# Deformable sampling as TensorE products with hat weights instead of row gathers, on one Trainium2 core

## The chip, the cores and the metric

The kernel runs on one core of one Trainium2 chip. The metric is the device time of one execution in microseconds (us). In the profile PE is TensorE's matmul, PEld its weight load, DVE is VectorE, ACT is ScalarE, POOL is GpSimd, SP is SyncE; a "q" behind a name (SPq) is that engine's DMA queue. The clock in a table is the share of its full clock that TensorE was granted. "L369" is line 369 of that kernel's own source, so the same statement has other numbers in the variants below.

## The reference

Two layers over `x` of shape [2, 256, 128, 128], all fp32. The first normalises `x` by groups, computes for three branches (dilation 1, 9, 12) offsets by a 3x3 convolution, samples the image bilinearly at nine shifted taps, weights the taps per channel, and applies a LayerNorm over the channels and a gelu. The sum of the branches and of a 1x1 convolution passes through a LayerNorm, an MLP and a last LayerNorm. The second layer is a ternary 3x3 convolution.

```python
def _deform_dw(x, offset, w, pad, dil):
    off = offset.reshape(B, 9, 2, H, W)
    py = yy - pad + ky * dil + off[:, :, 0]
    px = xx - pad + kx * dil + off[:, :, 1]
    sampled = _bilinear(x, py, px)                 # 4 corners per tap, zero outside the image
    return jnp.einsum('bckhw,ck->bchw', sampled, w.reshape(C, 9))

def _branch(x, w_off, w_def, lw, lb, pad, dil):
    off = _conv(x, w_off, pad, dil)
    y = _deform_dw(x, off, w_def, pad, dil)
    return gelu(_ln2d(y, lw, lb))                  # LayerNorm over the 256 channels of a pixel
# ... (cut)
out = _ln2d(x1 + x2 + x3 + conv1x1(x), n1_w, n1_b)
out = _ln2d(mlp(out) + out, n2_w, n2_b)
```

## The kernel before

Pixels lie on the 128 partitions, channels along the free axis. For each of 27 taps of each image row, one indirect DMA on GpSimd gathers the four corners of 128 pixels (4 KB each) from a table. ACT and DVE blend them with per-pixel weights, DVE multiplies by the tap's weights, and TensorE adds the nine taps in PSUM.

```python
# per tap (phase_b), 2 x 128 x 27 = 6912 times
nc.scalar.activation(s, G[:, 0:C], AF.Copy, scale=wt[:, 0:1])
for j in range(1, 4):
    nc.vector.scalar_tensor_tensor(s, G[:, j * C : (j + 1) * C], wt[:, j : j + 1], s, ALU.mult, ALU.add)
nc.vector.tensor_tensor(sw, s, defw[:, tap, :], ALU.mult)
ins = nc.tensor.matmul(y, lhsT=ident, rhs=sw, start=kt == 0, stop=kt == 8)
advance()      # one step of LayerNorm, gelu and MLP of an earlier row
```

With pixels on the partitions a LayerNorm needs one number for each partition, so the inverse square root runs on GpSimd over one column:

```python
def rsqrt(dst, var, eps):
    nc.gpsimd.tensor_scalar(ve, var, eps, None, ALU.add)
    nc.gpsimd.tensor_tensor(dst, ve, mhalf[:, :n], ALU.pow)      # n = 1 (2 for group norms)
```

The offsets of image 1 and the last convolution of image 0 are traced beside the sampling (`together`); the rest of the kernel is not needed here.

Of the kernel before, what the change touches and what calls it, by code (L numbers as in the profile page):

```python
# [10 lines left out]
I32 = mybir.dt.int32  # L11
# [10 lines left out]
KC = C // P          # channel chunks  # L22
HID = 512
MC = HID // P
R = 4                # image rows per group
NG = R * W           # pixels per group
PAD = 12             # widest reach of the offset convolutions
WP = W + 2 * PAD
DILS = (1, 9, 12)
NTAP = 27            # 3 branches x 9 taps  # L30
NOFF = 2 * NTAP
NPLAN = 5 * NTAP     # 4 corner weights and one index per tap
TW = W + 2           # the sampling table has a row per (floor(y) + 1, floor(x) + 1)
AHEAD = 7            # gathers issued ahead of the tap that uses them
GBUFS = 9
LOAD_AT = 64         # the tap of a group at which the next group's loads are issued
# [3 lines left out]
# 0.05 in float32, its two 12-bit halves, and half a unit in its last place  # L40
# [7 lines left out]
def conv_preact_kernel(ctx: ExitStack, tc: tile.TileContext, t: dict, out: bass.AP):  # L48
    nc = tc.nc
    x = t["x"]  # L50
    NB, _, H, _ = x.shape
    NGRP = H // R
    HALO = PAD // R      # groups of rows on either side that an offset convolution reaches
    TH = H + 2
# [3 lines left out]
    small = ctx.enter_context(tc.tile_pool(name="small", bufs=6))  # L58
    ps_tp = ctx.enter_context(tc.tile_pool(name="ps_tp", bufs=2, space=PSUM))
    ps_mm = ctx.enter_context(tc.tile_pool(name="ps_mm", bufs=2, space=PSUM))  # L60

# [1 line left out]
    ident = const.tile([P, P], F32, name="ident")  # L63
    make_identity(nc, ident)
    mhalf = const.tile([P, 2], F32, name="mhalf")
    nc.vector.memset(mhalf, -0.5)
    ones = const.tile([1, P], F32, name="ones")
    nc.vector.memset(ones, 1.0)

    def load(name, shape, src):  # L70
# [5 lines left out]
    offw = load("offw", [P, KC, 9, NOFF], t["offw"].rearrange("(k p) t n -> p k t n", p=P))  # L76
# [3 lines left out]
    convb = load("convb", [1, C], t["convb"])  # L80
    b2 = load("b2", [1, C], t["b2"])
    b1 = load("b1", [P, MC], t["b1"])
    n1w = load("n1w", [P, KC], t["n1w"])
# [4 lines left out]
    defw = load("defw", [P, NTAP, C], t["defw"].partition_broadcast(P))  # L88
    bw = load("bw", [P, 3, C], t["bw"].partition_broadcast(P))
    bb = load("bb", [P, 3, C], t["bb"].partition_broadcast(P))  # L90

# [1 line left out]
    table = [  # L93
        scratch.tile([TH * TW, 4 * C], F32, name=f"table{b}", tag=f"table{b}") for b in range(NB)
    ]
    plan = [scratch.tile([H, W, NPLAN], F32, name=f"plan{b}", tag=f"plan{b}") for b in range(NB)]
    x1d = [scratch.tile([C, H * W], F32, name=f"x1d{b}", tag=f"x1d{b}") for b in range(NB)]

    # Work for TensorE that runs beside a main stream is issued behind this instruction of it.
    fence = None  # L100

    def behind(ins):
        if fence is not None:
            tc.add_manual_dep(
                ins.ins,
                fence.name,
                mybir.DependencyInfo(
                    mybir.DependencyClass.NoSync, mybir.DependencyReason.DATA
                ),
                reason="beside the main stream",  # L110
            )

# [1 line left out]
    def rsqrt(dst, var, eps):  # L114
        """dst = (var + eps) ** -0.5"""
        n = var.shape[1]
        ve = small.tile([P, n], F32, name="ve", tag="ve")
        nc.gpsimd.tensor_scalar(ve, var, eps, None, ALU.add)  # L118
        nc.gpsimd.tensor_tensor(dst, ve, mhalf[:, :n], ALU.pow)  # L119

    def group_norm(stats, name):
        """Per channel mean and rstd of its group of 8 channels; stats [P, KC, n, 6]."""
        mv = small.tile([P, KC, 2], F32, name="gnmv", tag="gnmv", bufs=2)
        for k in range(KC):
            nc.vector.bn_aggr(mv[:, k, :], stats[:, k].rearrange("p n s -> p (n s)"))  # L125
        mean = const.tile([P, KC], F32, name=f"{name}_mean", tag=f"{name}_mean")
        rstd = const.tile([P, KC], F32, name=f"{name}_rstd", tag=f"{name}_rstd")
        pm = ps_mm.tile([P, 512], F32, name="gnps", tag="mm")
        nc.tensor.matmul(pm[:, 0:KC], lhsT=gmask, rhs=mv[:, :, 0], start=True, stop=True)
        nc.vector.tensor_copy(mean, pm[:, 0:KC])  # L130
        d = small.tile([P, KC], F32, name="gnd", tag="gnd", bufs=2)
        nc.vector.tensor_tensor(d, mv[:, :, 0], mean, ALU.subtract)
        nc.vector.tensor_tensor(d, d, d, ALU.mult)
        nc.vector.tensor_tensor(d, d, mv[:, :, 1], ALU.add)
        pv = ps_mm.tile([P, 512], F32, name="gnps", tag="mm")
        nc.tensor.matmul(pv[:, 0:KC], lhsT=gmask, rhs=d, start=True, stop=True)
        var = small.tile([P, KC], F32, name="gnvar", tag="gnvar", bufs=2)
        nc.vector.tensor_copy(var, pv[:, 0:KC])
        rsqrt(rstd, var, GN_EPS)
        return mean, rstd  # L140

    def ln_stats(src):
        """Mean and rstd of each row of src [P, C]."""
        st = small.tile([P, 6], F32, name="lnst", tag="lnst")
        nc.vector.bn_stats(st, src)  # L145
        mv = small.tile([P, 2], F32, name="lnmv", tag="lnmv")
        nc.vector.bn_aggr(mv, st)  # L147
        rs = small.tile([P, 1], F32, name="lnrs", tag="lnrs")
        rsqrt(rs, mv[:, 1:2], LN_EPS)
        return mv, rs  # L150
# [3 lines left out]

    gn1 = []
    with tc.tile_pool(name="gnload", bufs=2) as gp:
        XT = min(8, NGRP)
        for b in range(NB):
            stats = gp.tile([P, KC, NGRP, 6], F32, name="stats1", tag="stats1")
            for k in range(KC):  # L160
                for g0 in range(0, NGRP, XT):
                    n = min(XT, NGRP - g0)
                    xt = gp.tile([P, XT * NG], F32, name="xt", tag="xt")
                    nc.sync.dma_start(
                        xt[:, : n * NG],
                        x[b, k * P : (k + 1) * P].rearrange("p h w -> p (h w)")[
                            :, g0 * NG : (g0 + n) * NG
                        ],
                    )
                    for j in range(n):  # L170
                        nc.vector.bn_stats(stats[:, k, g0 + j, :], xt[:, j * NG : (j + 1) * NG])
            gn1.append(group_norm(stats, f"gn1_{b}"))

# [1 line left out]
    def phase_a(b, pool, ps_off, ring, base):  # L175
        mean, rstd = gn1[b]
        tv = table[b].rearrange("(y x) (s c) -> y x s c", x=TW, s=4)

        # The border of the table, where a corner lies outside the image.
        zero = base["zero"]  # L180
        for dy in range(2):
            for yy in (0, H + 1) if dy == 0 else (H, H + 1):
                row = tv[yy, :, 2 * dy : 2 * dy + 2, :].rearrange("(q j) s c -> q j (s c)", j=2)
                for j in range(2):
                    nc.sync.dma_start(row[:, j], zero[0 : TW // 2])
            for dx in range(2):
                for xx in (0, W + 1) if dx == 0 else (W, W + 1):
                    nc.sync.dma_start(
                        tv[1 - dy : 1 - dy + H, xx, 2 * dy + dx, :], zero[0:H, 0:C]
                    )  # L190
        yield

        def load_group(g):
            for k in range(KC):
                nc.sync.dma_start(
                    ring[g % len(ring)][:, k, :, PAD : PAD + W],
                    x[b, k * P : (k + 1) * P, g * R : (g + 1) * R, :],
                )

        def normalise_group(g):  # L200
            for k in range(KC):
                xk = ring[g % len(ring)][:, k, :, PAD : PAD + W]
                normalise(xk, xk, mean[:, k : k + 1], rstd[:, k : k + 1])

        def tabulate(g):
            xp = ring[g % len(ring)]
            ts = pool.tile([P, R, C], F32, name="ts", tag="ts", bufs=2)
            for h in range(R // 2):
                tp = ps_tp.tile([P, 512], F32, name="tpa", tag="tp")
                for j in range(2):  # L210
                    for k in range(KC):
                        behind(
                            nc.tensor.transpose(  # L213
                                tp[:, (j * KC + k) * P : (j * KC + k + 1) * P],
                                xp[:, k, 2 * h + j, PAD : PAD + W],
                                ident,
                            )
                        )
# [547 lines left out]
```

## Time and profile before

| | us |
|---|---|
| median time (19012.79 to 19031.13) | 19021.79 |
| offsets of image 0, TensorE alone | to about 2400 |
| sampling of both images, DVE 81 to 87% busy | about 15,500 |
| last convolution of image 1 | about 1,070 |

### The profile page before, as it was taken

How to read it: one execution, taken by the hardware profiler on the slowest of the kernel's cores; microseconds unless marked ns; L12 is line 12 of the kernel's file. 1: busy time of each engine (PE TensorE's matmuls, PEld its weight loads, DVE VectorE, ACT ScalarE, POOL GpSimd, SP SyncE). 2: the span in 40 equal slices, each digit the busy share in tenths (PEclk: the TensorE clock that was granted, in tenths of full speed). 3: DMA queues.
4: the chain of work that ended last, by engine and by line, in shares of the span. 5: the costliest groups of instructions: out<-in, count | busy, mean ns of one | idle time of the engine just before them, and what ended most of it. 6: DMA issues, size and time to landing. Idle time of an engine off the chain costs nothing. (4 is left out here: it accounts for less than half of the span.)

```text
span 19048.3 us, 184576 instructions
## 1 busy us (share of the span) xinstructions
PE 15534.4 (82%) x52208; PEld 10999.5 (58%) x52208; DVE 13137.0 (69%) x35538; ACT 4065.9 (21%) x8322; POOL 9696.9 (51%) x9511
## 2 busy tenths in 40 slices
PE   7999998898989988888666677777777777777799
PEld 7999997777777777776333333333333344333344
DVE  2000017878777878888888888888888888888600
ACT  0000002222222222222222222222222222222100
POOL 0000005656555565666666666666666666666400
PEclk9855555666666666666666677777877777787899
DMA  4110127777777777777777777777778787888511
GB/s 145 32 40 31 37 71 241 244 243 251 241 245 245 241 247 247 245 242 248 262 259 260 244 257 262 260 263 258 261 259 263 257 264 260 267 263 261 179 39 37
DMA packets 1347582, 4036.18 MB, mean 212 GB/s; under 512 B 126946, under 2 KB 392292, under 8 KB 1344116
## 3 DMA queue, kind: packets, MB, share of 16 engines
q0 software_dynamic: 995328, 3624.32, 58.2%
q1 hardware_dynamic: 216052, 265.81, 4.1%
q10 hardware_dynamic: 135168, 134.23, 2.1%
q8 instruction: 408, 6.68, 0.1%
q14 instruction: 626, 5.13, 0.1%
HBM read 3800.61 MB, written 223.25 MB: 211 GB/s over the span
## 5 line engine op out<-in xcount | busy, mean ns | idle before, releaser
L359 POOL DMA_INDIRECT G<-table,plb x6912 | 8428.6, 1219 | 7312.3 <-DVE sw L502 2651.4
L498 DVE SCALAR_TENSOR_TENSOR s<-G,plb,s 128x256 f32<-128x256 f32 x20736 | 8855.1, 474 | 92.3 <-ACT s L496 90.4
L505 PE MATMUL y<-sw,ident 128*128 128x256 f32 x13824 | 6050.8, 552 | 2851.1 <-DVE sw L502 2841.0
L505 PEld LDWEIGHTS y<-sw,ident 128*128 128x128 f32 x13824 | 3141.6, 260 | 5205.4 <-DVE sw L502 4533.5
L496 ACT ACTIVATE s<-G,plb 128x256 f32<-128x256 f32 x6912 | 3414.4, 506 | 10383.7 <-DVE sw L502 10285.2
L248 PEld LDWEIGHTS po<-offw,ring 128*128 128x128 f32 x24544 | 5112.8, 311 | 192.5 <-issue 16.3
L248 PE MATMUL po<-offw,ring 128*128 128x18 f32 (+1 forms) x24544 | 4895.1, 356 | 4.0 <-DVE pos L281 4.0
L502 DVE TENSOR_TENSOR sw<-s,defw 128x256 f32<-128x256 f32 x6912 | 2807.5, 415 | 1.9
L609 PE MATMUL pc<-cring,wq 128*128 128x512 f32 x4608 | 2526.9, 694 | 55.5 <-DVE o L621 53.1
L270 DVE TENSOR_TENSOR pos<-po,pos 128x27 f32<-128x27 f32 x256 | 32.6, 177 | 2528.2 <-PE po L248 2528.2
L609 PEld LDWEIGHTS pc<-cring,wq 128*128 128x128 f32 x4608 | 1040.2, 227 | 1111.6 <-issue 929.1
L145 DVE BATCH_NORM_STATS2 lnst<-y 128x6 f32<-128x256 f32 x768 | 329.3, 429 | 939.0 <-PE y L505 930.5
L118 POOL TENSOR_SCALAR ve<-lnmv 128x1 f32<-128x1 f32 x1280 | 462.0, 361 | 762.7 <-DVE lnmv L147 689.5
L153 DVE TENSOR_SCALAR a<-y,lnmv,lnrs 128x256 f32<-128x256 f32 x768 | 416.3, 542 | 626.2 <-POOL lnrs L119 621.7
L119 POOL TENSOR_TENSOR lnrs<-ve,mhalf 128x1 f32<-128x1 f32 x1280 | 798.3, 624 | 67.3
L403 PE MATMUL S<-ge,ident 128*128 128x256 f32 x1536 | 734.3, 574 | 82.0 <-ACT ge L402 69.6
L621 DVE SCALAR_TENSOR_TENSOR o<-pc,l1b,xl 128x512 f32<-128x512 f32 x128 | 95.5, 746 | 840.7 <-PE pc L609 840.7
L219 ACT COPY ts<-tpa 128x512 f32<-128x512 f32 x128 | 74.1, 586 | 2500.5 <-PE tpa L213 2487.8
L438 PE MATMUL hp<-oT,w 128*128 128x512 f32 x1024 | 569.0, 681 | 0.7 <-ACT oT L424 0.7
L403 PEld LDWEIGHTS S<-ge,ident 128*128 128x128 f32 x1536 | 373.9, 279 | 335.5 <-ACT ge L402 246.8
L461 PE MATMUL h<-w,hT 128*128 128x256 f32 x2048 | 524.5, 389 | 0.0
L379 PE MATMUL S<-convb,ones 1*128 1x256 f32 x512 | 280.5, 644 | 207.5 <-DVE n L153 198.7
(98 smaller groups left out, 5523.1 us busy)
## 6 DMA issues: line engine op xcount, KB each, us to landing
table<-ts ACTq DMA_DIRECT2D x256, 512.0 KB, 6.8
G<-table,plb POOLq DMA_INDIRECT x6912, 5.5
xl<-x1d SPq DMA_DIRECT2D x120, 384.0 KB, 6.9
xt<-in_x SPq DMA_DIRECT2D x16, 2048.0 KB, 7.3
ring<-in_x SPq DMA_DIRECT2D x128, 256.0 KB, 3.9
xg<-in_x SPq DMA_DIRECT2D x64, 512.0 KB, 8.3
x1d<-x SPq DMA_DIRECT2D x64, 512.0 KB, 5.0
out_x<-o SPq DMA_DIRECT2D x128, 256.0 KB, 2.1
```

The source lines that it names most:

```text
L118: nc.gpsimd.tensor_scalar(ve, var, eps, None, ALU.add)
L119: nc.gpsimd.tensor_tensor(dst, ve, mhalf[:, :n], ALU.pow)
L248: nc.tensor.matmul(po[:, r * NOFF + n0 : r * NOFF + n0 + n], lhsT=xp[:, k, yy % R, PAD + dx : PAD + dx + W], rhs=offw[:, k, tap, n0 : n0 + n],
L359: nc.gpsimd.indirect_dma_start(out=G, out_offset=None, in_=table[b], in_offset=bass.IndirectOffsetOnAxis(ap=groups[g]["plan"][:, r, 4 * NT ...
L403: nc.tensor.matmul(gr["S"][r], lhsT=ident, rhs=ge, start=False, stop=br == 2)
L438: nc.tensor.matmul(hp, lhsT=w1[:, k, m * P : (m + 1) * P], rhs=oT[:, k, :], start=k == 0, stop=k == KC - 1,)
L461: nc.tensor.matmul(h2, lhsT=hT[:, m, cols], rhs=w2[:, m, :], start=False, stop=m == MC - 1)
L496: nc.scalar.activation(s, G[:, 0:C], AF.Copy, scale=wt[:, 0:1])
L498: nc.vector.scalar_tensor_tensor(s, G[:, j * C : (j + 1) * C], wt[:, j : j + 1], s, ALU.mult, ALU.add)
L502: nc.vector.tensor_tensor(sw, s, defw[:, tap, :], ALU.mult)
L505: ins = nc.tensor.matmul(y, lhsT=ident, rhs=sw, start=kt == 0, stop=kt == 8)
L609: nc.tensor.matmul(pc, lhsT=wq[:, k, ky * 3 + kx, m * P : (m + 1) * P], rhs=xc[:, k, ky : ky + R, kx : kx + W], start=i == 0, stop=i == KC ...
```

## The change

The intent is to replace gathers and DVE blending by matrix products. A source tile is 16 x 8 pixels on the partitions (128) by 256 channels. For an inner block of 10 columns by 2 rows and all nine taps, a matrix `A` [128 source pixels, 18 x 10] holds the product of two hat functions, max(0, 1 - |distance|) in y and in x. One product of tile and `A` samples the block at nine taps. This works while offsets are at most 3; a flag read at run time selects a branch with gathers otherwise. The largest offset of these inputs is 2.80, so the branch with products runs. ACT evicts the products (copies them out of PSUM, the memory that TensorE writes to), DVE adds the taps with per-channel weights into a ring of image rows.

Channels now lie on the partitions. A LayerNorm over channels becomes a product with a constant matrix of 1/256, which leaves the variance of 512 pixels in 512 columns, equal on all partitions, and the power runs over all of them. Nothing is interleaved any more: statistics, offsets with hat weights, sampling, last convolution follow each other.

The core of the diff (cut; the rest is the hat weights, the fallback and the order of stages):

```diff
-            nc.gpsimd.indirect_dma_start(out=G, ..., in_=table[b], in_offset=...)      # cut
-            nc.scalar.activation(s, G[:, 0:C], AF.Copy, scale=wt[:, 0:1])
-            for j in range(1, 4):
-                nc.vector.scalar_tensor_tensor(
-                    s, G[:, j * C : (j + 1) * C], wt[:, j : j + 1], s, ALU.mult, ALU.add
-                )
-            nc.vector.tensor_tensor(sw, s, defw[:, tap, :], ALU.mult)
+                        nc.tensor.matmul(
+                            pm[:, j, 0 : n * CI],
+                            lhsT=xts[brs, Rt][T // (NT // 2)][
+                                :, T % (NT // 2), c * P : (c + 1) * P
+                            ],
+                            rhs=A[:, m0:m1, AO + T * CI : AO + (T + 1) * CI],
+                            start=True,
+                            stop=True,
+                        )
+                    nc.scalar.copy(ev[...], pm[...])                                      # cut
+                        nc.vector.scalar_tensor_tensor(dst, src, w, dst, ALU.mult, ALU.add)
...
-        nc.gpsimd.tensor_tensor(dst, ve, mhalf[:, :n], ALU.pow)
+            for c in range(KC):
+                nc.vector.tensor_tensor(v[:, c, :], v[:, c, :], pm, ALU.subtract)
+            sq = pool.tile([P, KC, NG], F32, name="sq", tag="sq", bufs=2)
+            nc.scalar.activation(sq, v, AF.Square)
+            pv = psum.tile([P, 512], F32, name="lnv", tag="st", bufs=2)
+            for c in range(KC):
+                nc.tensor.matmul(
+                    pv, lhsT=mean_w, rhs=sq[:, c, :], start=c == 0, stop=c == KC - 1
+                )
+            rs = pool.tile([P, NG], F32, name="rs", tag="rs", bufs=2)
+            nc.scalar.activation(rs, pv, AF.Identity, bias=eps_t)
+            nc.gpsimd.tensor_tensor(rs, rs, mhalf, ALU.pow)
+            for c in range(KC):
+                nc.vector.tensor_tensor(v[:, c, :], v[:, c, :], rs, ALU.mult)
```

## The prediction

> **What bounds the kernel now.** I read four views, in this order: the page's busy shares and slices, the busy table by stages, the groups by form, and the waits with a stretch of the timeline. First the slices and the stages. The columns of the second fence are: stretch, its length, then busy us and count of PE, PEld, DVE, ACT and POOL, then granted TensorE clock, DMA share, GB/s.
>
> ```profile
> PE 15534.4 (82%) x52208; PEld 10999.5 (58%) x52208; DVE 13137.0 (69%) x35538; ACT 4065.9 (21%) x8322; POOL 9696.9 (51%) x9511
> ...
> DVE  2000017878777878888888888888888888888600
> ...
> PEclk9855555666666666666666677777877777787899
> ```
>
> ```profile
> 1428.00:1904.00 476.00, 476.00 (x2236) 476.00 (x2235) 24.56 (x125) 5.86 (x10) 0.00 (x0) 0.50 0.10 31
> ...
> 2857.00:9500.00 6643.00, 5798.25 (x21804) 4594.62 (x21803) 5364.62 (x14688) 1686.42 (x3464) 3998.96 (x3942) 0.62 0.75 246
> 9500.00:17500.00 8000.00, 5677.36 (x14518) 3086.53 (x14519) 6984.39 (x18568) 2194.65 (x4499) 5357.58 (x5207) 0.75 0.79 260
> ...
> 18100.00:19020.00 920.00, 872.78 (x2000) 373.30 (x2000) 1.00 0.12 39
> ```
>
> PE's 82% misleads. There are three stages. Up to 2.4 ms TensorE alone makes offsets with 18-column products at clock 0.50. From 2.4 to 17.95 ms the sampling runs: DVE is 81% busy to 9.5 ms and 87% after. The last 1.07 ms is the second image's 3x3 convolution on TensorE at clock 1.00. So 15.5 of 19.0 ms are the sampling. Next, what one of its taps costs:
>
> ```profile
> L498 DVE SCALAR_TENSOR_TENSOR s<-G,plb,s 128x256 f32<-128x256 f32 x20736 | 8855.1, 474 | 92.3 <-ACT s L496 90.4
> L359 POOL DMA_INDIRECT G<-table,plb x6912 | 8428.6, 1219 | 7312.3 <-DVE sw L502 2651.4 <-DMA table<-ts 2310.5 <-DVE s L498 1028.6
> ...
> L502 DVE TENSOR_TENSOR sw<-s,defw 128x256 f32<-128x256 f32 x6912 | 2807.5, 415 | 1.9
> ...
> L119 POOL TENSOR_TENSOR lnrs<-ve,mhalf 128x1 f32<-128x1 f32 x1280 | 798.3, 624 | 67.3
> ...
> L118 POOL TENSOR_SCALAR ve<-lnmv 128x1 f32<-128x1 f32 x1280 | 462.0, 361 | 762.7 <-DVE lnmv L147 689.5 <-DVE s L498 8.3 <-DVE pos L270 2.0
> ...
> L119 POOL TENSOR_TENSOR gn_rstd<-ve,mhalf 128x2 f32<-128x2 f32 x4 | 3.1, 784 | 0.3
> ```
>
> ```profile
> 12003.30 1.66 DVE L498 SCALAR_TENSOR_TENSOR s<-G,plb,s 128x256 f32<-128x256 f32 x4
> ...
> 12006.81 1.22 POOL L359 DMA_INDIRECT G<-table,plb  x1 [0.31 <-DVE s L498]
> ```
>
> A tap takes 15.55 ms / 6912 = 2.25 us; back to back, DVE gives it three products at 1.66/4 = 0.415 us and one at 0.75/2 = 0.38 (two of L502 in a row, elsewhere in the timeline), 1.62 together, and LayerNorm work on top. GpSimd waits for DVE's buffers (2651 and 1029 us), not DVE for gathers. DVE is the bound; its largest own wait is for the LayerNorm's small powers on GpSimd:
>
> ```profile
> DVE a L153 <- POOL lnrs L119: 621.7, 557, 4.5
> ```
>
> [...](packets, MB, share of 16 engines' time): the table's stores are 993 B in 47 ns each, so 16 engines could move 336 GB/s.
>
> ```profile
> q10 hardware_dynamic: 135168, 134.23, 2.1%
> ```
>
> [...]
>
> **The change, part by part.** The largest offset of the inputs, which I computed from the reference, is 2.80, so the branch without gathers runs. Counts are from the changed kernel's instruction lists. TensorE costs come from the last stretch: an fp32 product is two records, so these 36 are 18 products of 512 columns in 15.72 us, 0.873 us each or 1.705 ns a column at full clock.
>
> ```profile
> 18299.78 15.72 PE L609 MATMUL pc<-cring,wq 128*128 128x512 f32 x36 [0.84 <-DVE o L621]
> ```
>
> [...]the 18-column products took 427 ns at clock 0.50 (476 us for half of 2236 records), so 213 at full.
>
> Removed: 6912 gathers, 20736 + 6912 DVE operations, the interleaving of stages, the four-fold table. [...]
>
> *Statistics* of the input: about 0.13 ms, as now (PE is busy 345 of the first 476 us, so it starts near 131 us).
>
> *Offsets and hats.* 512 transposes at 0.22, 512 products of 486 columns at 0.83, 936 shifts at 0.24, 256 transposes at 0.22, 576 products of 512 at 0.87: 0.11+0.42+0.22+0.06+0.50 = 1.3 ms of TensorE; at a clock of 0.9, **1.45 ms**. DVE has about 0.55 and ACT 0.65 ms beside it. Now the first image's share alone takes 2.3 ms.
>
> *Sampling*, 402 steps:
> - TensorE: 9576 products of 180 columns at 0.307 and 1568 smaller at 0.22 = 3.3 ms; 2560 products of 512 columns for means, variances and MLP at 0.873 = 2.2 ms. **5.5 ms** at full clock, 6.5 at 0.85.
> - DVE: 5656 accumulations of some 256 elements at 0.415, 616 short and 788 first ones at about 0.3 = 2.77 ms; 1114 hat products of 768 elements at 0.90[...] = 1.0; LayerNorm subtractions and products, 1280 of 512 at 0.68 = 0.87; the rest of the tail 0.6. **5.2 ms**, against 12.7 now in 2.86 to 17.95 ms.
> - ACT: 3184 evictions of up to 720 elements, 0.76 for the largest (0.586 for 512 now[...]) = 2.1, plus 1.2 for the tail: 3.3 ms.
> - DMA: 3752 tiles of 128 KB, 2228 hat blocks of 384 KB and 0.17 GB more = 1.54 GB; at 330 GB/s 4.7 ms. Some 6700 issues at 0.46 us on one queue (first loads of the trace) = 3.1 ms.
> - GpSimd: 320 powers of **512 columns** instead of 1280 of one. The second column added 784 - 624 = 160 ns. Taken straight, 512 columns cost 82 us and all of them 26 ms.[...] This is the one number I can't take from a row.
>
> Each power lies in a chain: subtract on DVE, square on ACT 1.0, two products 1.7, bias on ACT 0.7, the power P, multiply on DVE. DVE is in order, and in the instruction list there lie some 9 to 12 accumulations (4.5 us) between subtract and multiply for the 192 branch norms, fewer for the 64 first row norms, none for the 64 last. So DVE stalls about 192 x (P-1) + 64 x (P+1) + 64 x (P+4) us. P = 1: 0.5 ms; P = 10: 3.3; P = 20: 6.5; P = 82: 26.
>
> I choose P near 10. One and two columns show the loop at its worst, where nothing overlaps; a long loop should overlap its iterations, which makes a few times less than 160 ns a column plausible, and it would be odd to widen the power to 512 columns if each took 80 us. That is a judgement, not a reading. Sampling: 5.2 of DVE work + 3.3 of stalls + 1 for waits on loads and products = **9.5 ms**.
>
> *Last convolution*: 2304 products at 0.873 = 2.0, plus weights: **2.1 ms**. The first image's half was hidden; now both halves are bare.
>
> Sum: 0.13 + 1.45 + 9.5 + 2.1 = **13.2 ms**.
>
> **Rivals.**
> (a) GpSimd becomes the bound. For: the 160 ns of the second column, 320 serial powers, DVE waiting already now for the one-column form. Against: only two sizes seen. At 82 us: 5.2 + 26 + 1 + 3.7 = 36 ms, slower; the break with 19.0 ms lies near P = 28.
> (b) TensorE or DMA sets the pace. With a cheap power, TensorE at 0.85 has 6.5 ms and DMA 4.7 to 5.7: sampling 7 ms, in all 10.7. For: PE and DVE sums are close, so buffers of two may couple them. Against: nothing here holds TensorE 100% busy.
> (c) One queue carries all loads and stores in order; a store that waits for a late tail holds back the tiles and hats behind it. It adds to the stalls of (a), 1 to 2 ms; the present trace has some 700 such transfers and shows the queue waiting for data, not DVE for loads.
>
> **Range and chances.** 10.8 ms is a cheap power and rival (b); 17.5 ms is P = 20 with rival (c). Rival (a) in full gets about 1 in 8. Faster 0.87, within 2% 0.01, slower 0.12.
>
> **What would show it.** Mean time of the 512-column power (10 us; over 28 breaks the prediction); DVE's idle time before the multiply, put down to GpSimd (about 3 ms); DVE busy 5.2 ms and clock above 0.8 in the sampling; 0.41 us per accumulation, 0.76 per eviction, 0.87 per 512-column product; first stages over by 1.6 ms; the last convolution in 2.1. It is wrong if the power is linear in columns, if evictions with runs of 10 elements are slower than dense ones, or if the 1 KB and 3 KB loads run well below 300 GB/s.

## The result, and the profile after

The changed kernel takes 37566.16 us (37550.97 to 37578.44, 4 runs), the kernel before 19021.79 us in the same rounds. The ratio is 1.9748 (95% interval 1.972 to 1.9776). Ratios here are the mean time of one kernel's fast runs over that of the other's of the same rounds, so not quite the ratio of the medians quoted. The change makes the kernel almost twice as slow. The measured time lies far outside the predicted range; it lies by what the prediction called rival (a), "GpSimd becomes the bound", which it had put at 36 ms.

The page of the changed kernel, its busy shares, two rows of its slices, and the engines' shares in the chain of work that ended last:

```profile
PE 10374.7 (28%) x36848; PEld 6722.4 (18%) x36848; DVE 5954.4 (16%) x11715; ACT 3649.3 (10%) x5554; POOL 26306.1 (70%) x332
...
POOL 0167777787878778788767777878787777878700
PEclk9866666555555565555566566555555555555599
...
POOL 68%; issue 19%; PE 5%; DVE 0%; DMA 0%; ACT 0%; SPq 0%; POOLq 0%; ACTq 0%; DVEq 0%
```

Every other engine is mostly idle: DVE fell from 69% to 16% and from 13.1 to 6.0 ms. GpSimd has only 332 counted instructions and is busy for 26.3 ms. TensorE's clock sits at 0.5 to 0.6 in the middle (e2, which takes the waits away, has 0.92 there). "issue" is time for which the profile shows no releaser. The groups by form show which instruction it is (columns: busy us, mean ns; then idle time before it and what ended it):

```profile
L369 POOL TENSOR_TENSOR rs<-rs,mhalf 128x512 f32<-128x512 f32 x320 | 26301.9, 82193 | 7845.3 <-ACT rs L368 7373.9 <-DVE ring L589 238.1 <-DMA hy<-hats 233.3
...
L619 ACT COPY ev<-pm 128x720 f32<-128x720 f32 x2052 | 1548.0, 763 | 2343.2 <-PE pm L610 1943.5 <-DVE ring L589 309.3 <-issue 64.5
...
L371 DVE TENSOR_TENSOR ring<-ring,rs 128x512 f32<-128x512 f32 x384 | 248.3, 688 | 15712.3 <-POOL rs L369 15712.3
```

One power over 512 columns takes 82.19 us. The waits (us in total, times, longest) show that it holds up not only the multiply behind it but, through DVE's order and the buffers, all engines:

```profile
DVE ring L371 <- POOL rs L369: 15712.3, 192, 88.0
ACT ge L380 <- DVE ring L371: 15637.2, 192, 83.0
...
PE pm L610 <- ACT ev L619: 13831.2, 708, 87.6
DVE S L371 <- POOL rs L369: 10747.6, 128, 87.8
```

A stretch of the timeline (start, duration, engine, instruction, idle time before and releaser) shows one of these chains whole:

```profile
12745.49 82.14 POOL L369 TENSOR_TENSOR rs<-rs,mhalf 128x512 f32<-128x512 f32 x1 [14.73 <-ACT rs L368]
...
12827.67 1.29 DVE L371 TENSOR_TENSOR S<-S,rs 128x512 f32<-128x512 f32 x2 [80.64 <-POOL rs L369]
12828.40 1.52 ACT L433 ACTIVATE S<-S,n1b,n1w 128x512 f32<-128x512 f32 x2 [81.09 <-DVE S L371]
...
12829.26 9.19 PE L441 MATMUL hp<-S,w 128*128 128x512 f32 x16 [80.66 <-ACT S L433]
```

The multiply, the activation behind it and the products behind that each waited 81 us, the same 81 us. The power before it (from 12647.85 us) shows the order of the work on DVE and ACT. DVE ran nothing from 12648.76 us to its multiply at 12730.79. The additions that came next (L586, 12732.01) were of values that ACT had copied by 12648.80. The next copies (L619, 12732.94) stood behind the gelu (12731.52), though by the profile their products had ended by 12651.46. Last, the busy table by stages (length; busy us and count of PE, PEld, DVE, ACT, POOL; TensorE clock, DMA share, GB/s), for the offsets with hats, the sampling and the last convolution:

```profile
130.00:1434.00 1304.00, 1298.38 (x4805) 611.69 (x4803) 462.86 (x956) 476.66 (x830) 0.38 (x1) 0.99 0.44 124
1434.00:35540.00 34106.00, 7086.11 (x27408) 5233.19 (x27408) 5176.69 (x10234) 3170.20 (x4721) 26291.35 (x320) 0.60 0.17 45
35540.00:37565.00 2025.00, 1983.49 (x4616) 872.63 (x4616) 227.35 (x373) 0.00 (x0) 12.31 (x4) 0.99 0.12 43
```

Of 37.6 ms, 34.1 are the sampling stage. DVE's work in it is 5.18 ms.

### The profile page after: what moved, and what is told of

It reads as the page before. It is cut to its first block, busy times and chain, and to the rows that moved or that the text cites. A ratio compares the mean times of both kernels' runs of the same rounds, so it can differ in the third digit from the quotient of the medians.

```text
span 37565.0 us, 108286 instructions
## 1 busy us (share of the span) xinstructions
PE 10374.7 (28%) x36848; PEld 6722.4 (18%) x36848; DVE 5954.4 (16%) x11715; ACT 3649.3 (10%) x5554; POOL 26306.1 (70%) x332
## 4 chain that ended last, share of the span: by engine, by line
POOL 68%; issue 19%; PE 5%; DVE 0%; DMA 0%; ACT 0%; SPq 0%; POOLq 0%; ACTq 0%; DVEq 0%
POOL rs L369 68%; PE pc L843 5%; PE pm L610 0%; DVE ring L589 0%; DMA hx<-hats 0%; ACT ev L619 0%; SPq L496 0%; DMA xn<-in_x 0%; ACT ge L380 0%; PE lnm L355 0%; DVE up L786 0%; DMA wq<-in_l1w 0%; DVE A L550 0%; DVE wq L810 0%; POOLq L369 0%
## 5 line engine op out<-in xcount | busy, mean ns | idle before, releaser
L369 POOL TENSOR_TENSOR rs<-rs,mhalf 128x512 f32<-128x512 f32 x320 | 26301.9, 82193 | 7845.3 <-ACT rs L368 7373.9
L610 PE MATMUL pm<-A,xs 128*128 128x180 f32 (+2 forms) x22288 | 4506.3, 363 | 15855.9 <-ACT ev L619 13831.2
L610 PEld LDWEIGHTS pm<-A,xs 128*128 128x128 f32 x22288 | 4169.1, 220 | 16502.1 <-ACT ev L619 14124.9
L589 DVE SCALAR_TENSOR_TENSOR ring<-ev,defw,ring 128x256 f32<-128x256 f32 (+5 forms) x6272 | 2647.4, 468 | 89.0 <-ACT ev L619 43.9
L619 ACT COPY ev<-pm 128x720 f32<-128x720 f32 (+2 forms) x3184 | 2025.4, 659 | 2945.3 <-PE pm L610 2373.8
L364 PE MATMUL lnv<-sq,mean_w 128*128 128x512 f32 x1280 | 790.0, 749 | 5482.7 <-ACT sq L361 5479.6
L441 PE MATMUL hp<-S,w 128*128 128x512 f32 x1024 | 602.5, 754 | 5189.0 <-ACT S L433 5189.0
L843 PE MATMUL pc<-cring,wq 128*128 128x512 f32 x4608 | 1981.2, 592 | 17.1 <-DVE wq L810 16.9
L380 ACT ACTIVATE ge<-ring,bb,bw 128x512 f32<-128x512 f32 x384 | 291.5, 806 | 15637.2 <-DVE ring L371 15637.2
L550 DVE TENSOR_TENSOR A<-hy,hx 128x768 f32<-128x768 f32 x1130 | 1107.0, 984 | 898.0 <-DMA hx<-hats 573.3
L256 PE MATMUL ph<-planes,hatw 62*72 62x512 f32 x1152 | 550.8, 616 | 2.9 <-ACT hb L264 2.0
```

The source lines that it names most:

```text
L256: nc.tensor.matmul(ph[0:NH], lhsT=k["hatw"][0:NPLANE, q * NH : (q + 1) * NH], rhs=pl[0:NPLANE, :], start=True, stop=True,)
L364: nc.tensor.matmul(pv, lhsT=mean_w, rhs=sq[:, c, :], start=c == 0, stop=c == KC - 1)
L369: nc.gpsimd.tensor_tensor(rs, rs, mhalf, ALU.pow)
L441: nc.tensor.matmul(hp, lhsT=w1[:, c, m * P : (m + 1) * P], rhs=S[:, c, :], start=c == 0, stop=c == KC - 1,)
L550: nc.vector.tensor_tensor(dst, hy[:, :, i0 * W : i1 * W].rearrange("p t (i w) -> p t i w", w=W), hx[:, :, i0 * W : i1 * W].rearrange("p t ...
L589: nc.vector.scalar_tensor_tensor(dst, src, w, dst, ALU.mult, ALU.add)
```

## The experiments

Theory A: each power costs 160 ns a column and lies whole in a serial chain, so the time is a constant plus 320 times the power. Rivals: a fixed cost in the power (B); other work hidden under the stalls that would come out when they shrink (C). The first four ran on one chip, beside runs of the kernel before at 19098.84 us. The runs with a wrong result (e1, e2, e4, e6) are single runs; the others are four runs each.

### e1: the power over half the columns (wrong result)

```diff
-            nc.gpsimd.tensor_tensor(rs, rs, mhalf, ALU.pow)
+            nc.gpsimd.tensor_tensor(rs[:, 0:256], rs[:, 0:256], mhalf[:, 0:256], ALU.pow)
```

> Power over the first 256 of the 512 columns only (wrong result on purpose). Theory A, each power is linear in its columns (160 ns each) and sits whole in a serial chain on DVE's in-order path: one power 41 us, DVE idle before the multiply down by about 192 x 41 + 128 x 41 = 13 ms, total 37.6 - 13.1 = 24.4 ms. Rival B, the power has a large fixed part or the loop gets cheaper only when short: 60 us or more, total above 30 ms. Rival C, other work of the sampling stage that the stalls now cover shows up when they shrink: total clearly above 24.4 although the power is at 41 us.

Measured: 24408.49 us. The group of the power in e1:

```profile
L369 POOL TENSOR_TENSOR rs<-rs,mhalf 128x256 f32<-128x256 f32 x320 | 13210.1, 41282 | 7763.5 <-ACT rs L368 7316.1
```

(82193 - 41282) / 256 = 159.8 ns a column. The kernel became faster by (37570.00 - 24408.49) / 320 = 41.13 us per power (37570.00 is e4, the full-width power on this chip) and the power by 40.91. All of it is paid. (e4 is a single run of a variant; its 37570.00 agrees with the 37566.16 of the changed kernel.)

### e2: an add instead of the power (wrong result)

```diff
-            nc.gpsimd.tensor_tensor(rs, rs, mhalf, ALU.pow)
+            nc.gpsimd.tensor_tensor(rs, rs, mhalf, ALU.add)
```

> The same GpSimd instruction with an add in place of the power, 512 columns (wrong result on purpose). Theory A: the add takes 1 to 1.5 us[...], total 37.6 - 320 x 81 us = 11.7 ms. Rival C, TensorE with its 5.5 ms at full clock, the one load queue or the buffers of two set a floor under the sampling stage: total 13 ms or more, and the line through this point and the half power is bent.

Measured: 11344.41 us. The group of the add, and the sampling stage in the table by stages, in e2:

```profile
L369 POOL TENSOR_TENSOR rs<-rs,mhalf 128x512 f32<-128x512 f32 x320 | 426.1, 1332 | 7477.6 <-ACT rs L368 6764.2
```

```profile
1434.00:9350.00 7916.00, 6515.24 (x27443) 4798.70 (x27441) 5210.46 (x10278) 3162.53 (x4733) 427.56 (x322) 0.92 0.75 196
```

The same instruction with the same operands and another operation takes 1.33 us. From e1 the kernel lost (24408.49 - 11344.41) / 320 = 40.83 us per power for 39.95 us of the instruction. So the line through 82, 41 and 1.3 us is straight to within 2%: A holds, and nothing came out from under the stalls (not C). Without the price of the power the whole change would be a gain.

### e3: the power over 4 columns (correct)

All partitions held the same 512 numbers. With the operands of the variance product exchanged, pixels go to the partitions and the power has 4 columns. TensorE spreads the result over the channels again.

```diff
-                nc.tensor.matmul(
-                    pv, lhsT=mean_w, rhs=sq[:, c, :], start=c == 0, stop=c == KC - 1
-                )
+            for j in range(R):
+                for c in range(KC):
+                    nc.tensor.matmul(pv[:, j : j + 1], lhsT=sq[:, c, j * P : (j + 1) * P],
+                                     rhs=mean_w[:, 0:1], start=c == 0, stop=c == KC - 1)
-            nc.scalar.activation(rs, pv, AF.Identity, bias=eps_t)
-            nc.gpsimd.tensor_tensor(rs, rs, mhalf, ALU.pow)
+            nc.vector.tensor_scalar(r4, pv[:, 0:R], LN_EPS, None, ALU.add)
+            nc.gpsimd.tensor_tensor(r4, r4, mhalf[:, 0:R], ALU.pow)
+            for j in range(R):
+                nc.scalar.activation(dg[:, j, :], ident, AF.Copy, scale=r4[:, j : j + 1])
+            for j in range(R):
+                nc.tensor.matmul(rs[:, j * P : (j + 1) * P], lhsT=ones_w, rhs=dg[:, j, :],
+                                 start=True, stop=True)
```

> A correct remedy: the variance products give [128 pixels, 4], the power runs on 4 columns, and TensorE spreads it over the channels again as a product of ones with diagonal matrices that ACT makes. Theory A: the power takes 0.3 + 4 x 0.16 = about 1.0 us, the chain is longer by 4 small ACT operations (0.3 us each) and 4 small products (0.2 us each): about 3 us a norm more than with the add, 320 x 3 = 1 ms at most; total 12 to 13 ms, faster than both kernels. Rival B (a fixed cost of GpSimd's power of tens of us) would leave it above 19 ms.

Measured: correct, 11944.69 us (11928.49 to 11950.64), ratio to the kernel before 0.6254 (0.6244 to 0.6265). The power and the sampling stage in e3:

```profile
L376 POOL TENSOR_TENSOR r<-r,mhalf 128x4 f32<-128x4 f32 x320 | 359.6, 1124 | 8140.4 <-DVE r L375 7862.6 <-DMA hx<-hats 229.8 <-DVE ring L604 48.0
```

```profile
1434.00:9920.00 8486.00, 7125.74 (x33824) 5778.43 (x33822) 5106.32 (x10567) 3350.29 (x5689) 358.62 (x319) 0.88 0.70 183
```

The power takes 1.12 us, so it has no fixed cost of tens of us (not B). The total lies just under the 12 to 13 ms expected. The detour costs (11944.69 - 11344.41) / 320 = 1.9 us a norm against e2. This kernel beats both.

### e4: the power over 512 columns of one partition (wrong result)

```diff
-            nc.gpsimd.tensor_tensor(rs, rs, mhalf, ALU.pow)
+            nc.gpsimd.tensor_tensor(rs[0:1], rs[0:1], mhalf[0:1], ALU.pow)
```

> Power over all 512 columns but of one partition only (wrong result on purpose). If the cost goes by columns and the 128 partitions are worked on side by side (theory A, which says that laying pixels across partitions is the remedy): 82 us again, total 37.6 ms. If the cost goes by elements (rival): the power falls by 16 or more, to 5 us or less, and the total to about 13 ms.

Measured: 37570.00 us, and the power in e4:

```profile
L369 POOL TENSOR_TENSOR rs<-rs,mhalf 1x512 f32<-1x512 f32 x320 | 26298.8, 82184 | 7846.8 <-ACT rs L368 7353.6
```

One partition costs what 128 cost. The price goes by columns, not by elements.

### e5: square root on ACT and reciprocal on DVE (correct)

Without any power:

```diff
-            nc.scalar.activation(rs, pv, AF.Identity, bias=eps_t)
-            nc.gpsimd.tensor_tensor(rs, rs, mhalf, ALU.pow)
+            nc.scalar.activation(rs, pv, AF.Sqrt, bias=eps_t)
+            nc.vector.reciprocal(rs, rs)
```

> Another correct remedy with no power at all: ACT takes the square root of the variance (512 columns), DVE the reciprocal. The cause named (only the price of the power on GpSimd) says any cheap replacement will do: ACT pays two switches of its function set per norm, some 2.6 us[...], 320 x 2.6 = 0.8 ms of an engine that is busy 3.2 of 7.9 ms, plus a reciprocal of 0.7 us on DVE[...]; total 11.5 to 12.5 ms. If the reciprocal is several times slower than that, say 3 us, 320 x 2.5 = 0.8 ms more, since DVE stalls are paid in the chain.

Measured: correct, 11750.11 us (11746.85 to 11757.49), ratio 0.6175 (0.6164 to 0.6185). In e5 the groups of the reciprocal and of the loads of a function set (`ACT_TABLE_LOAD`) at the square root (L368) and at the gelu of a branch (L380):

```profile
L369 DVE RECIPROCAL rs<-rs 128x512 f32<-128x512 f32 x320 | 1071.5, 3348 | 107.1 <-ACT rs L368 106.9
...
L368 ACT ACT_TABLE_LOAD x257 | 329.7, 1283 | 4.5
L380 ACT ACT_TABLE_LOAD x192 | 246.3, 1283 | 3.4
```

The changed kernel has two such loads in all, e5 has these 449. Each takes 1283 ns, two take 2.57 us, so the 2.6 us expected for two switches are the loads alone; ACT stood idle for 4.5 us in all before the 257 and 3.4 us before the 192. The reciprocal takes 3.35 us, where a subtraction or product of that size takes 0.67 to 0.68 (e5, 673 and 684 ns): the slow case of the expectation. In ratios e5 lies 0.024 above e2 (0.594), 1.4 us a norm, less than the 2.6 us of the two loads at a branch norm and the 2 us that the reciprocal takes over the add: here a part of the longer chain was hidden. The remedy is still the simplest one: two lines.

### e6 to e12: what the sampling stage runs at once the power is cheap

The prediction gave this stage 6.2 ms without stalls of the power (5.2 of DVE work plus 1 of waits); e2 has 7.9, of which DVE waited 0.6 for the short add. e6 and e7, then e8 to e11, then e12 came on three chips, and e3 on a fourth, so I compare ratios to the kernel before. Across chips such ratios are good to some 0.4% only: on the chip of e1 to e4 the kernel before was 0.4% slower than in the first rounds, and the full-width power (e4) was not. "Theory A" in e6 and e7 is another one: TensorE sets the stage.

**e6**, on e3, drops two of three column taps from DVE's additions (`for kx in (0, -1, 1)` becomes `for kx in (0,)`, wrong result).

> On the kernel with the narrow power: only the middle column tap of each row of taps is accumulated, about 3080 of 6272 DVE accumulations fewer, 1.4 ms of DVE's 5.1 (wrong result on purpose). Theory A, with the power gone TensorE is what the sampling stage runs at (7.1 of 8.5 ms busy at clock 0.88): total falls by less than 0.4 ms, to 11.6 or so. Rival, the prediction's own sum, DVE work plus its waits set the stage: total falls by 1.4 ms to 10.5.

Measured: 11652.34 us, ratio 0.6124 against 0.6254 of e3, so about 0.25 ms less. In the sampling stage of e6 DVE is busy 3.31 ms instead of 5.11:

```profile
1434.00:9630.00 8196.00, 7025.30 (x33806) 5746.82 (x33805) 3310.88 (x5863) 3359.12 (x5689) 362.49 (x319) 0.88 0.72 189
```

DVE lost 1.8 ms of work and the stage 0.3, so DVE's work is not what sets the stage, and the prediction's sum of DVE work and waits does not hold there. A part of what was cut came back as waits: DVE's hat products waited 1591 us for the loads of hat blocks (`hx`), in e3 568.

**e7**, on e3, makes table, source tiles and hat products bf16:

```diff
+BF16 = mybir.dt.bfloat16
-    table = dram("table", [HT * WT, C])
+    table = [scratch.tile([HT * WT, C], BF16, name=f"table{b}", tag=f"table{b}") for b in range(NB)]
-            ts = pool.tile([P, R, C], F32, name="ts", tag="ts", bufs=2)
+            ts = pool.tile([P, R, C], BF16, name="ts", tag="ts", bufs=2)
# ... likewise the tiles zero, xs, A and, in the fallback, G
```

> On the kernel with the narrow power: source tiles and hat weights of the sampling products in bf16 instead of fp32 (table, tiles, hat products); everything else stays fp32. [...]the sampling products go from 4.4 to about 1.2 ms, and the tile loads from 0.49 to 0.25 GB. Theory A, TensorE bound: the sampling stage falls from 8.5 ms to where DVE with its waits is, 6 to 7 ms, total 9.5 to 10.5 ms. Rival, DVE bound: total stays within 0.3 ms of 11.9. Correctness of the output is open: the tolerance may not allow bf16 here.

Measured: correct, 11843.41 us (11832.52 to 11872.80), ratio 0.6229 (0.6218 to 0.624). The sampling stage of e7:

```profile
1434.00:9820.00 8386.00, 5226.05 (x22669) 3353.61 (x22667) 4999.20 (x10561) 3282.33 (x5684) 362.85 (x320) 0.66 0.61 155
```

TensorE's busy time fell by 1.9 ms, the stage by 0.1. (The largest group of sampling products fell from 3920.6 to 1565.4 us, to 40%; the expectation had 4.4 to 1.2 ms for all of them, the author's estimate, which this run does not bear out. The clock fell from 0.88 to 0.66.) TensorE is not the bound either, though e3 shows it 84% busy. My theory for e6 and e7 was wrong, although e6 had come out as it said: a forecast that is met does not show its cause.

**e8 to e11** test the loads: more buffers (source tiles 3 to 5, hat blocks 3 to 6, e8), the tail's transfers moved from the SyncE queue to GpSimd's (e9), both (e10), and the queue edit on the fp32 kernel e3 (e11).

```diff
-            xt = pool.tile([P, NT // 2, C], BF16, name="xs", tag="xs", bufs=3)
+            xt = pool.tile([P, NT // 2, C], BF16, name="xs", tag="xs", bufs=5)      # e8, e10
# hy and hx: bufs 3 to 6                                                             # e8, e10
-                nc.sync.dma_start(g12d[b]..., ge)
+                nc.gpsimd.dma_start(g12d[b]..., ge)                                  # e9, e10, e11
# likewise g12, xn, xr and x1d
```

> On the bf16 kernel, which took TensorE's sampling work down by 1.9 ms of busy time and gained only 0.1: buffers for source tiles 3 to 5 and for hat blocks 3 to 6, nothing else. Theory L, the loads of the next step start too late because their buffers are freed only in the middle of the step: sampling 8.4 to about 6.5 ms, total 9.5 to 10.5 ms. Rival Q, the one in-order load queue is blocked by stores and by loads whose buffer waits for the tail: less than 0.3 ms gain from buffers alone.

> On the bf16 kernel: the tail's stores and loads (g12d, g12, xn, xr, x1d; 320 transfers of 0.5 MB) are issued from GpSimd instead of the SyncE queue, buffers as they were. Rival Q: the queue no longer waits for products and activations of the tail (744 + 331 + 221 us of its waits), total falls by about 1 ms or more, to 10.5 to 10.9. Theory L: less than 0.3 ms.

> Both edits on the bf16 kernel. If L and Q each hold a part: total 9 to 10 ms, and DVE, 5.0 ms busy in the sampling stage, is next. If neither is the cause, 11.5 to 11.9 ms again.

> The queue edit alone on the all-fp32 kernel with the narrow power. If TensorE (7.1 of 8.5 ms busy) is close to being the bound there, the gain is smaller than on the bf16 kernel: 0 to 0.7 ms, total 11.2 to 11.9.

| run | us (range) | ratio to before (95%) |
|---|---|---|
| e3, fp32 | 11944.69 (11928.49 to 11950.64) | 0.6254 (0.6244 to 0.6265) |
| e11, e3 + queue | 11761.03 (11733.77 to 11775.58) | 0.6187 (0.6177 to 0.6198) |
| e7, bf16 | 11843.41 (11832.52 to 11872.80) | 0.6229 (0.6218 to 0.624) |
| e8, e7 + buffers | 11686.10 (11673.71 to 11696.18) | 0.6144 (0.6134 to 0.6154) |
| e9, e7 + queue | 11664.56 (11659.73 to 11669.37) | 0.6133 (0.6123 to 0.6143) |
| e10, e7 + both | 11383.12 (11371.33 to 11400.71) | 0.5986 (0.5976 to 0.5996) |

Each is correct. e8, e9 and e10, on another chip than e7, lie below it by 1.4%, 1.5% and 3.9% of its ratio: small, but more than the 0.4% between chips. e11 is below e3 by 1.1%. Neither L nor Q has the size that I had expected; e11 came out as expected. In e10 the queue's own timeline in the pass over one branch shows something else:

```profile
2014.62 0.54 SPq L546 DMA_DIRECT2D hy<-hats  x1
2015.21 0.60 SPq L546 DMA_DIRECT2D hx<-hats  x1
2015.91 12.75 SPq L514 DMA_DIRECT2D xs<-table  x14
2028.76 0.54 SPq L546 DMA_DIRECT2D hy<-hats  x1
```

The queue issues without a break: 14 source tiles in 12.75 us (0.9 us each) and six hat blocks in 3.5, 16 us for a step. e8, the base of e12, has the same pattern there: 14 tiles in 12.00 us.

**e12**, on e8, issues half of the source tiles from GpSimd:

```diff
-                    nc.sync.dma_start(xt[:, T, :], src)
+                    (nc.gpsimd if t0 else nc.sync).dma_start(xt[:, T, :], src)
```

> On the bf16 kernel with the deeper buffers (11.69 ms): the second half of each row of source tiles is issued from GpSimd, the first half and the hat blocks stay on the SyncE queue. In the pass over one branch that queue issues without a break, 14 tiles at 0.9 us and 6 hat blocks at 0.6 us, 16 us a step. Theory S, issue time on one queue sets this pass: 134 steps shrink to about 11 us, 0.7 ms off, total 11.0 ms. Rival D, the 16 DMA engines are nearly full there (share 0.79) or the step waits elsewhere: less than 0.2 ms off.[...]

Measured: correct, 11211.41 us (11201.60 to 11220.13), ratio 0.5895 (0.5885 to 0.5905), the best of all. The next pass of image 0 begins with the first load of `xn`; its first and last start, in e8 and then in e12:

```profile
L419 SPq DMA_DIRECT2D xn<-in_x x64: 373/374/645, 2785.5 to 9361.8; - x64
```

```profile
L419 SPq DMA_DIRECT2D xn<-in_x x64: 373/374/669, 2523.1 to 8875.9; - x64
```

The pass over one branch became 0.26 ms shorter, twice that for two images, which is what e12 gained (0.47 ms) to within 0.05. Theory S holds for this pass, with two thirds of the size expected. Whether the 0.9 us are issue time alone or also a queue that is held back was not tested; one queue was the limit either way. It may not be far from the next one: from 1434 to 2500 us the DMA engines are 72% busy in e8 and 87% in e12.

What sets the longer pass over two branches stays **open**. It is not DVE's work alone (e6) nor TensorE's alone (e7); the waits of e3 and e7 are spread over many small ones. Both cuts at once, which would test whether the engines hold each other up through their few buffers, were not run, and neither was a cut in the bytes of the hat blocks.

## Why the prediction was wrong, point by point

- **The step that failed** is the price of the power: "I choose P near 10." Measured: 82.19 us (e4: 82.18; half the columns 41.28). The prediction had the straight reading of the profile before, 160 ns for the second column, hence 82 us, and set it aside with the thought that "a long loop should overlap its iterations". e1 shows no such gain: 159.8 ns a column between 256 and 512, as between one and two.
- The second ground for the choice, "it would be odd to widen the power to 512 columns if each took 80 us", was an argument about the author of the change and rested on no reading of a trace.
- **The mechanism was right.** The stall formula, 192 x (P - 1) + 64 x (P + 1) + 64 x (P + 4), gives 26.4 ms at P = 82.2; DVE's waits for GpSimd before the multiply are 15.71 + 10.75 = 26.46 ms. Rival (a) in full said 36 ms; measured 37.57. Its chance was put at 1 in 8, although the only slope pointed to it.
- **The second mis-sized term** is the "1 for waits on loads and products" in the sampling stage. Without the power the stage was to take 6.2 ms. The changed kernel has 34.1 - 26.46 = 7.6, and e2 has 7.92 - 0.60 = 7.3 (the stall formula gives 0.55 for its 1.33 us). DVE's work was right (5.2 against 5.18), so the waits are 2.1 to 2.5 ms instead of 1, and e6 shows that less work of DVE turns mostly into more waiting. Rival (b) had this stage at 7 ms, low too, with TensorE or DMA as its cause; e7 did not bear out TensorE.
- **The loads ran slower than the 330 GB/s assumed.** In e2's sampling stage the DMA engines moved 196 GB/s at a busy share of 0.75, which makes about 261 GB/s if they were always busy (an estimate from that line). The 1.55 GB then take 5.9 ms of their time, not 4.7. The prediction had named "well below 300 GB/s" as a sign of being wrong.
- Rival (c), one queue for all loads and stores, is real but small beside the 1 to 2 ms it was given: about 1.5% (e9) and 1.1% on fp32 (e11). Splitting the issue of the loads, which it had not named, gave 4% (e12 against e8).
- The break-even the prediction named, P near 28, is close to the line from e1 to e2: with 40.8 us of time per 40 us of power, 19.0 ms is reached at about 25 us.
- Right within a few per cent: 0.76 us for the largest eviction (763 ns; against 459 ns for 360 columns that is 0.84 ns a column), 0.68 us for a subtraction or product of 512 columns (680 to 688 ns; 679 for the residual add of the kernel before), 3.3 ms of ACT in the sampling (3.17), 2.1 ms for the last convolution (2.03). The offsets took 1.30 ms at clock 0.99; the forecast was 1.45 at 0.9. The clock in the sampling was 0.60, not above 0.8; in e2, with 0.60 ms of stalls instead of 26.46, it was 0.92.
- **Readings of the trace before that were wrong without effect on the result.** DVE's largest wait was not for the powers (621.7 and 307.0 us in two rows) but for the offset products (2528.2 us), and the one for the tap sums (930.5 us) was as large as the powers. The offset products ran at clock 1.00 and 0.83 in the first two stretches of 476 us and at 0.50 after that. TensorE finished as many records at 0.83 as at 0.50 (2249 and 2236), so "213 at full" does not follow from 427 ns at 0.50. It was busy for all 476 us of three stretches at clock 0.50, so being busy did not bring it a higher clock there.

## What to carry to other kernels

When a layout change moves a small operation from one column to hundreds, price that operation again from the profile, and take the slope that two sizes show rather than the one that would be comfortable. The power on GpSimd cost by columns and not by partitions (82.18 us on one partition, 82.19 on 128, 1.12 for 4 columns), so put the numbers across the partitions (e3) or use a square root and a reciprocal (e5). A helper instruction in a chain can be paid in full: here every microsecond of the power between 1.3 and 82 us appeared in the total, 320 times (41.13 us for 40.91 of the power, then 40.83 for 39.95), and DVE stood idle for 26.46 ms before the multiplies behind it. In e5, at a few microseconds, only a part was paid.

## Prices measured in this case

- A power on GpSimd: 82.19 us for 512 columns, 41.28 for 256 (e1), 1.12 for 4 (e3), and 82.18 on one partition (e4); 159.8 ns a column between 256 and 512. An add of 512 columns took 1.33 us (e2).
- DVE's reciprocal of 128x512 fp32: 3.35 us, against 0.67 to 0.68 for a subtraction or product of that size (e5).
- An fp32 product of 512 columns: two records and 0.873 us at clock 1.00 (kernel before); the weight load of such a record took 189 ns (changed kernel, last convolution).
- Loads: 14 tile loads in a row held one queue for 12.75 us of a 16 us step (e10), and issuing half of them from GpSimd took 4% off the kernel (e8 to e12).
